# A slot-ordered selective scan on one core: the gate put behind a scan, the D skip and one sum put a slot later

## The chip, the cores and the metric

The kernel runs on one core of a Trainium2 chip. The metric is device time in microseconds (us) of one execution. Before the change the median of three runs is 5206.82 us (5206.63 to 5207.61). One further execution was profiled; every duration below that is not a run time comes from its trace.

## The reference, cut to what matters

Two images of 256 channels by 4096 positions go through two layers. Layer 0 holds one Mamba block (256 inner channels); layer 1 holds two, one forward and one over the reversed positions (512 inner channels each), and then a mixture of 8 expert networks. The heart of every Mamba block is a recurrence with 16 states for each channel, a sum over the states, a skip by `D`, and a gate by `silu(z)`:

```
def step(h, inp):
    dt_t, B_t, C_t, x_t = inp
    h = h * jnp.exp(dt_t[..., None] * A) + (dt_t * x_t)[..., None] * B_t[:, None, :]
    y = jnp.einsum('bds,bs->bd', h, C_t)
    return (h, y)
...
y = sw(ys) + xc * D
out = y * _silu(z) @ W_out
```

All arithmetic is float32.

## The kernel before, in words

**Tiling.** Positions are cut into 8 chunks of 512 (`T`). A channel tile is 128 channels, so a chunk of layer 0 has `nj` = 2 tiles and one of layer 1 has `nj` = 4. The 16 states of a tile are handled in four groups of four. One such group is a *quad*: a buffer `bq` of 128 partitions (32 channels times 4 states) by four channel sets by 512 positions. Six `bq` buffers exist (`bqp`), so quad m takes the buffer of quad m - 6. A quad is worked in two halves `h` of 128x1024; each half is a *slot*. Eight quads, that is 16 slots and two channel tiles, make a *block*. The whole loop (L1011 and below) has 640 quads, 1280 slots, 80 blocks: 8 blocks for layer 0 of image 0, 16 for the forward and 16 for the backward block of layer 1, and the same again for image 1. Slots are counted 0 to 15 inside a block here; slot 2n + h is the pair (n, h) of the code.

**What one quad needs.** GpSimd (POOL) multiplies the replicated `dt*x` by `B` into `bq` (`emit_b`, L654). ScalarE (ACT) puts `exp(dt*A)` of each half into a PSUM tile `da` (`emit_decay`, L664, two instructions of 128x512; there are two `da` tiles, so the one of slot s takes the place of slot s - 2). VectorE (DVE) scans the half (`emit_scan`, L690). The product with `C` is made by DVE right behind the scan (`emit_times_c`, L699) or, for quads n = 0, 2, 5 and in every second block half of n = 4, by POOL (`emit_times_c_quad`, L714 and L715; the two are called c0, c2, c5 and h4 here). TensorE (PE) sums the four states with the constant `stack` (`emit_sum`, L723) into the one PSUM bank `y` of the tile. Before the first sum of a tile the bank is opened with `D` times `xc` (`emit_skip`, L730); after its last sum DVE multiplies it into `sz`, the gate (`emit_gate`, L742). As `ps_y` has one buffer, a tile's skip must wait for the gate of the tile before it. `emit_diagonal` (L735) makes the skip's weights on ACT in slots 0 and 8.

**What sets the order.** Each engine works in the order in which the loop emits, which is kept by hand (`in_order`). In each slot the loop emits: the DMA list `sp`; the gate, when the slot is (1, 0) or (5, 0); the skip, when it is (1, 1) or (5, 1); the PE list `pe`; the sums that the table `SUMS` gives this slot; the PE list `pe2` (the experts); ACT's carry of the slot before (L709), the decay of the *next* slot (with its one-column join L675), and the list `act`; the list `dve0`; the scan; the list `dve`; the product with `C`; POOL's entries from `POOL_AT`. The lists hold the next chunk's preparation: input projections (`xs`, `z`, L414), convolution (L452) whose result goes through ACT's tanh (L461) and DVE's product (`xc`, L466), `dbc` (L481), `dt` (L501 to L523), and the finish of the chunk before, the output projection (`o`, L759 and L761). They share three PSUM banks (`psp`). In layer 0 the convolution stands in slot 12, the output projections in slots 7 and 8, and `xs` in slots 9 and 10.

**A planner** (`experts`, L847 and below) puts matmuls of the experts into slots where it reckons PE and ACT to have room; the cost that it takes for sums and skip of a slot is `sums_in`. What does not fit is done after the loop, in the last 680 us.

Of the kernel before, what the change touches and what calls it, by code (L numbers as in the profile page):

```python
# [61 lines left out]

POOL_HALF = (4, 0)

SUMS = {(0, 0): (-1,), (2, 0): (0, 1), (4, 0): (2, 3), (5, 1): (4,), (7, 0): (5, 6)}
POOL_AT = {0: "b3", 1: "c0 b4", 2: "b5", 3: "c2 b6", 4: "b7", 5: "h4 b8", 6: "c5 b9", 7: "b10"}
HUGE = 1e37

# [63 lines left out]
def hybrid_kernel(ctx: ExitStack, tc: tile.TileContext, a: dict, out: bass.AP):  # L132
# [53 lines left out]
    with ExitStack() as st:  # L186
# [394 lines left out]
        def at(g):  # L581

            i, jp, n = quads[g]
            return i, 2 * jp + n // SG, n % SG
# [48 lines left out]
        def flush(slot):  # L633
            for p in list(pending):
                if p[0] <= slot and (p[1] if len(p[1]) > 1 else p[1][0]) in cks[p[3]]:
                    pending.remove(p)
                    p[2]()
# [18 lines left out]
        def emit_decay(g, h):  # L656
            if g >= nq or ("rdt", at(g)[1]) not in cks[at(g)[0]]:
                return
            emit_join(g, h)
            i, j, sg = at(g)  # L660
            da[g, h] = ps_d.tile([P, 2, T], F32, tag="da", name=f"da_{g}_{h}")
            for k in range(2):
                q = 2 * h + k
                nc.scalar.activation(  # L664
                    da[g, h][:, k, :], cks[i]["rdt", j][:, q, :], AF.Exp,
                    scale=steps[i][0].w["a"][:, j, q * SG + sg : q * SG + sg + 1],
                )
# [12 lines left out]
        def on_pool(g, h):  # L680

            n = quads[g][2]
            return n in POOL_C or (n, h) == POOL_HALF and g // QN % 2

        def emit_scan(g, h):
            i, j, sg = at(g)
            job, c = steps[i]
            d = da[g, h].rearrange("p q t -> p (q t)")
            b = bq[g][:, 2 * h : 2 * h + 2, :].rearrange("p q t -> p (q t)")
            nc.vector.tensor_tensor_scan(  # L690
                b if on_pool(g, h) else d, d, b,
                job.h[:, j, sg, 2 * h : 2 * h + 1] if c else 0.0, ALU.mult, ALU.add,
            )
# [10 lines left out]
        def emit_carry(g, h):  # L704

            i, j, sg = at(g)
            d, two = da.pop((g, h)), slice(2 * h, 2 * h + 2)
            if not on_pool(g, h):
                nc.scalar.copy(steps[i][0].h[:, j, sg, two], d[:, :, T - 1])  # L709
# [10 lines left out]
        def emit_sum(g):  # L720
            i, j, sg = at(g)
            for q in range(SG):
                nc.tensor.matmul(  # L723
                    y[i, j][q * CG : (q + 1) * CG, :], stack, bq[g][:, q, :],
                    start=False, stop=(sg == SG - 1),
                )

        def emit_skip(i, j):
            y[i, j] = ps_y.tile([P, T], F32, tag="y", name=f"y_{i}_{j}")
            nc.tensor.matmul(y[i, j], diag.pop((i, j)), cks[i]["xc", j], start=True, stop=False)  # L730
# [9 lines left out]
        def emit_gate(i, j):  # L740
            sz = cks[i]["sz", j]
            nc.vector.scalar_tensor_tensor(sz, y.pop((i, j)), 0.5, sz, ALU.mult, ALU.mult)  # L742
# [104 lines left out]
        def experts():  # L847

            last = 2 * nq - 6
            banks = sorted(sl.banks, key=lambda r: r[0])  # L850

            def fits(slot):

                at = sum(b[0] <= slot for b in banks)
                both = banks[:at] + [(slot, slot + 1, 0)] + banks[at:]
                return all(
                    both[k - 3][1] + both[k][2] <= both[k][0] for k in range(max(3, at - 2), min(len(both), at + 4))
                    if at in range(k - 3, k + 1)
                )

            def sums_in(slot):
                n, h = divmod(slot % 16, 2)
                return 1.25 * len(SUMS.get((n, h), ())) + (1 if (n, h) in ((1, 1), (5, 1)) else 0)

            todo = [(at, b, c, e) for at, b, c in sorted(ready) for e in range(E)]
            behind = act_behind = 0.0
            times = [[], [], []]

            def follows(l):

                k, m = divmod(len(times[l]), KC)
                if k == len(todo):
                    return None
                waits = [(l - 1, k * KC + 1, 2)] if l else []
                if m:
                    waits.append((l, k * KC, 0))
                elif k:

                    waits.append((l, k * KC - 1, 6 if l == 0 and todo[k][-1] == 0 else 5))
                    if l < 2:  # L880
                        waits.append((l + 1, k * KC - 1, 0))
                if any(n >= len(times[w]) for w, n, _ in waits):
                    return None
                return max([todo[k][0] + 3] + [times[w][n] + d for w, n, d in waits])

            for slot in range(last):
                behind = max(0.0, behind) + sl.products.get(slot, 0) + sums_in(slot) - PE_ROOM
                act_behind = max(0.0, act_behind) + sl.acts.get(slot + 1, 0) - ACT_ROOM
                for l in (2, 1, 1, 0, 0):
                    at = follows(l)  # L890
                    if at is None or slot < at:
                        continue
                    if behind + 2 > PE_BEHIND or act_behind + 1.3 > ACT_BEHIND or not fits(slot):
                        break
                    banks.insert(sum(b[0] <= slot for b in banks), (slot, slot + 1, 0))
                    times[l].append(slot)
                    behind += 2
                    act_behind += 1 if l == 2 else 1.3
            put = [
                (*item[1:], [times[l][k * KC + m] for l in range(3) for m in range(KC)])  # L900
                for k, item in enumerate(todo) if (k + 1) * KC <= len(times[2])
            ]
            emit_experts(put)
# [106 lines left out]
        done = []  # L1010
        for g in range(nq):  # L1011
            i, jp, n = quads[g]
            for h in range(2):
                slot = 2 * g + h
                sl.run(slot, "sp")
                flush(slot)

                if (n, h) in ((1, 0), (5, 0)) and done:
                    emit_gate(*done.pop(0))

                if (n, h) in ((1, 1), (5, 1)):
                    emit_skip(i, 2 * jp + n // SG)
                sl.run(slot, "pe")
                for m in SUMS.get((n, h), ()):
                    if g - n + m >= 0:
                        emit_sum(g - n + m)
                sl.run(slot, "pe2")
                if (n, h) in ((0, 0), (4, 0)) and g:
                    done.append(at(g - 1)[:2])

                if slot:
                    emit_carry(*divmod(slot - 1, 2))
                emit_decay(*divmod(slot + 1, 2))
                if (n, h) in ((0, 0), (4, 0)):
                    emit_diagonal(i, 2 * jp + n // SG)
                sl.run(slot, "act")

                sl.run(slot, "dve0")
                emit_scan(g, h)
                sl.run(slot, "dve")  # L1040
                if not on_pool(g, h):
                    emit_times_c(g, h)

                if h == 0:
                    for what in POOL_AT.get(n, "").split():
                        m = g - n + int(what[1:])
                        if what[0] == "c":
                            emit_times_c_quad(m)
                        elif what[0] == "h":
                            if on_pool(m, 0):  # L1050
                                emit_times_c_quad(m, SG // 2)
                        else:
                            want_b(m)
                sl.run(slot, "pool")
            in_order()
# [6 lines left out]
    with ExitStack() as st:  # L1062
# [5 lines left out]
        n, x, y, acc, wts, wb, lt, w_dram = {}, {}, {}, {}, {}, {}, {}, {}  # L1068
# [192 lines left out]
        done = {i: 0 for i in rest}  # L1261
        count = {i: sum(p[1] == i for p in pairs) for i in rest}
        for at, (b, i, e) in enumerate(pairs):
# [3 lines left out]
            h = layer(n[b, i], 0, e, f"{i}_{e}_{b}")  # L1267
            h = layer(h, 1, e, f"{i}_{e}_{b}")
# [122 lines left out]
```

## Time and profile before

| what | value |
|---|---|
| median of three runs | 5206.82 us |
| the profiled execution's own time | 5213.06 us |
| its span, first to last instruction | 5211.3 us |
| busy in the span: DVE, POOL, PE, ACT | 4584.8, 4410.2, 4298.0, 3681.8 us |
| last gate of the loop | 4531.6 us after the start |
| gates (L742): number, median duration, DVE idle before them | 160, 0.682 us, 45.6 us |
| scans (L690) with a carried state: mean duration | 2.35 us |
| product by `B` on POOL (L654): number, mean | 640, 4.542 us |
| mean granted clock of TensorE | 0.918 |

In what follows, a line of a timeline gives the start in us from the first instruction, the duration in us, the engine, the line of the kernel, the operation, what it writes and reads, the shapes, how many instructions were merged (x), and in brackets how long the engine stood idle before it and what ended that. A line of waits gives who waited for whom, the sum in us, how many times, and the longest. A line by stretches gives from:to, its length, the busy us of PE, PE's weight loads, DVE, ACT and POOL with their numbers of instructions, then PE's granted clock, the DMA share and GB/s.

### The profile page before, as it was taken

The page shows a single profiled execution, that of the slowest core. Times are in us where ns is not written, and L with a number is a line of the kernel's source. Part 1 is how long each engine was busy: PE and PEld are TensorE (multiplying, and loading weights), DVE is VectorE, ACT ScalarE, POOL GpSimd, SP SyncE. Part 2 cuts the span into 40 slices and gives each one's busy share as a digit, 9 for nine tenths or more (in the row PEclk, how much of TensorE's full clock was granted, in tenths as well). Part 3 has the DMA queues.
Part 4 walks back from the last instruction along what each step waited for, and adds up shares of the span by engine and source line. Part 5 has one row for each costly group of instructions (what it writes and reads, how often), then busy time and mean ns, then how long its engine had stood idle before and what let it go on. Part 6 is the DMA issues. An engine that isn't in the chain of part 4 may idle for free. (4 is left out here: it accounts for less than half of the span.)

```text
span 5211.3 us, 47295 instructions
## 1 busy us (share of the span) xinstructions
PE 4298.0 (82%) x14920; PEld 1488.2 (29%) x14920; DVE 4584.8 (88%) x3083; ACT 3681.8 (71%) x7462; POOL 4410.2 (85%) x1438
## 2 busy tenths in 40 slices
PE   5777666766668888888888888888999989689999
PEld 1222212222222333332222332322333333234444
DVE  6998999999999999998989999999999999746333
ACT  5777777777767888887887888788788888522332
POOL 5998999999999999998989999999999999611010
PEclk8778888888889999999999999999999999899999
DMA  4444433344434554555555544445544455354322
GB/s 175 146 165 164 162 134 126 130 156 148 140 135 159 187 186 166 181 174 185 197 177 182 178 169 169 164 159 194 184 171 163 163 184 178 115 194 154 111 103 77
DMA packets 314731, 834.47 MB, mean 160 GB/s; under 512 B 35240, under 2 KB 102064, under 8 KB 272496
## 3 DMA queue, kind: packets, MB, share of 16 engines
q1 hardware_dynamic: 310768, 806.15, 44.5%
q0 software_dynamic: 3712, 25.30, 1.2%
q8 instruction: 118, 1.93, 0.1%
q14 instruction: 133, 1.09, 0.1%
HBM read 647.18 MB, written 184.16 MB: 160 GB/s over the span
## 5 line engine op out<-in xcount | busy, mean ns | idle before, releaser
L654 POOL TENSOR_TENSOR bq<-rxdt,bc 128x2048 f32<-128x2048 f32 x640 | 2892.9, 4542 | 34.8 <-issue 17.4
L664 ACT ACTIVATE da<-rdt,w_a 128x512 f32<-128x512 f32 x2560 | 1756.8, 686 | 113.6 <-DVE bq L690 67.8
L690 DVE TENSOR_TENSOR_SCAN da<-da,h_state,bq 128x1024 f32<-128x1024 f32 x664 | 1559.5, 2349 | 38.7 <-ACT da L664 27.3
L715 POOL TENSOR_TENSOR bq<-bq,bc 128x2048 f32<-128x2048 f32 (+1 forms) x280 | 1179.6, 4213 | 22.5
L723 PE MATMUL y<-bq,stack 128*32 128x512 f32 x5120 | 779.4, 687 | 362.1 <-POOL bq L715 337.2
L690 DVE TENSOR_TENSOR_SCAN bq<-da,h_state,bq 128x1024 f32<-128x1024 f32 x456 | 1052.3, 2337 | 27.9 <-ACT da L664 27.8
L699 DVE TENSOR_TENSOR bq<-da,bc 128x1024 f32<-128x1024 f32 x760 | 928.2, 1221 | 18.7
L912 PE MATMUL e<-eh,ew 128*128 128x512 f32 x1184 | 582.4, 621 | 60.5 <-DVE sp L513 20.5
L709 ACT COPY h_state<-da 128x2 f32<-128x2 f32 x759 | 119.3, 157 | 687.5 <-DVE bq L699 685.4
L675 ACT ACTIVATE bq<-h_state,bq,a 128x1 f32<-128x1 f32 x1120 | 429.9, 384 | 0.5
L723 PEld LDWEIGHTS y<-bq,stack 128*32 128x32 f32 x5120 | 144.9, 118 | 935.1 <-POOL bq L715 458.6
L1205 ACT ACTIVATE h<-hp,of,sc 128x512 f32<-128x512 f32 x216 | 167.7, 777 | 345.0 <-PE hp L1201 328.5
L414 PE MATMUL xs<-nx,w_in 128*128 128x512 f32 x640 | 320.1, 630 | 36.8 <-DVE xc L466 20.7
L414 PE MATMUL z<-nx,w_in 128*128 128x512 f32 x640 | 326.2, 638 | 23.7 <-DVE sp L513 16.9
L912 PEld LDWEIGHTS e<-eh,ew 128*128 128x128 f32 x1184 | 212.4, 193 | 422.3 <-issue 194.5
L912 PE MATMUL e<-en,ew 128*128 128x512 f32 x592 | 290.5, 622 | 47.3 <-DVE fcen L809 21.5
L452 PE MATMUL conv<-xs,w_conv 64*64 64x512 f32 x2560 | 320.5, 608 | 4.6 <-DVE sp L513 3.7
L761 PE MATMUL o<-sz,w_out 128*128 128x512 f32 x640 | 306.7, 620 | 0.0
L923 ACT ACTIVATE eh<-e,of,sc 128x512 f32<-128x512 f32 x296 | 223.7, 769 | 37.9 <-PE e L912 36.7
L517 POOL TENSOR_TENSOR xdt<-sp,xc 128x512 f32<-128x512 f32 x160 | 203.4, 1275 | 53.3 <-DVE sp L513 53.3
L501 PE MATMUL dt<-dbc,w_dt 64*128 64x512 f32 x320 | 197.2, 701 | 44.5 <-ACT dbc L488 27.7
L730 PE MATMUL y<-xc,w_d 128*128 128x512 f32 x320 | 181.0, 649 | 60.8 <-DVE sz L742 51.3
(138 smaller groups left out, 5043.0 us busy)
## 6 DMA issues: line engine op xcount, KB each, us to landing
rxdt<-xdtd SPq DMA_DIRECT2D x160, 1024.0 KB, 6.4
rdt<-dtd SPq DMA_DIRECT2D x160, 1024.0 KB, 6.3
bc<-bcd SPq DMA_DIRECT2D x384, 256.0 KB, 3.2
dtd<-sp SPq DMA_DIRECT2D x160, 256.0 KB, 3.5
xdtd<-xdt SPq DMA_DIRECT2D x160, 256.0 KB, 3.4
ew<-in_W SPq DMA_DIRECT2D x148, 256.0 KB, 4.8
u<-eu SPq DMA_DIRECT2D x74, 512.0 KB, 3.5
u<-u SPq DMA_DIRECT2D x74, 512.0 KB, 4.0
```

Source lines behind the costliest of these rows:

```text
L414: nc.tensor.matmul(ps, job.w["in", half][:, k, j * P : (j + 1) * P], rhs, start=(k == 0), stop=(k == KC - 1),)
L452: nc.tensor.matmul(v[r][64 * col : 64 * col + 64, :], job.w["conv"][rows, 2 * jp + j, k, :], ck["xs", jp][rows, j, k : k + T] if k < 4 els ...
L654: nc.gpsimd.tensor_tensor(bq[g], ck["rxdt", j], over_groups(ck["bc", 0, sg]), ALU.mult)
L664: nc.scalar.activation(da[g, h][:, k, :], cks[i]["rdt", j][:, q, :], AF.Exp, scale=steps[i][0].w["a"][:, j, q * SG + sg : q * SG + sg + 1],)
L675: nc.scalar.activation(bq[g][:, q, 0:1], job.h[:, j, sg, q : q + 1], AF.Identity, scale=cks[i]["a0", j][:, h, sg : sg + 1], bias=bq[g][:, ...
L690: nc.vector.tensor_tensor_scan(b if on_pool(g, h) else d, d, b, job.h[:, j, sg, 2 * h : 2 * h + 1] if c else 0.0, ALU.mult, ALU.add,)
L699: nc.vector.tensor_tensor(bq[g][:, two, :], d, cks[i]["bc", 1, sg].rearrange("p (o t) -> p o t", o=1).to_broadcast([P, 2, T]), ALU.mult,)
L715: nc.gpsimd.tensor_tensor(b, b, cks[i]["bc", 1, sg].rearrange("p (o t) -> p o t", o=1).to_broadcast([P, groups, T]), ALU.mult,)
L723: nc.tensor.matmul(y[i, j][q * CG : (q + 1) * CG, :], stack, bq[g][:, q, :], start=False, stop=(sg == SG - 1),)
L761: nc.tensor.matmul(v[m], job.w["out"][:, j, m * P : (m + 1) * P], ck["sz", j], start=False, stop=(j == job.nj - 1),)
L912: nc.tensor.matmul(ps, ew[l][:, k, m * P : (m + 1) * P], key[x][:, k, :], start=(k == 0), stop=(k == KC - 1),)
L923: nc.scalar.activation(key[dst][:, m, :], key["ps", l, m], AF.Relu, bias=of[:, l, e, m : m + 1], scale=sc[:, l, e, m : m + 1],)
```

## The change

Three edits. The gate is emitted behind the scan of its slot instead of ahead of it. The skip is emitted in slots 4 and 12 instead of 3 and 11; the sums 0 and 1 of a tile, which stood in slot 4 before, now follow it in the same slot. The sum of quad 4 goes from slot 11 to slot 12, where it follows the list `pe`. The planner's `sums_in` is told of it. Nothing is computed differently, and no instruction is added or taken away.

```
-SUMS = {(0, 0): (-1,), (2, 0): (0, 1), (4, 0): (2, 3), (5, 1): (4,), (7, 0): (5, 6)}
+SUMS = {(0, 0): (-1,), (2, 0): (0, 1), (4, 0): (2, 3), (6, 0): (4,), (7, 0): (5, 6)}
...
-                return 1.25 * len(SUMS.get((n, h), ())) + (1 if (n, h) in ((1, 1), (5, 1)) else 0)
+                return 1.25 * len(SUMS.get((n, h), ())) + (1 if (n, h) in ((2, 0), (6, 0)) else 0)
...
-                if (n, h) in ((1, 0), (5, 0)) and done:
-                    emit_gate(*done.pop(0))
-
-                if (n, h) in ((1, 1), (5, 1)):
+                if (n, h) in ((2, 0), (6, 0)):
                     emit_skip(i, 2 * jp + n // SG)
                 sl.run(slot, "pe")
...
                 sl.run(slot, "dve0")
                 emit_scan(g, h)
+
+                if (n, h) in ((1, 0), (5, 0)) and done:
+                    emit_gate(*done.pop(0))
                 sl.run(slot, "dve")
                 if not on_pool(g, h):
                     emit_times_c(g, h)
```

## Prediction

> **What bounds the kernel now.** I read the profile by stretches first, cut where the layers change: 60 to 538 us is layer 0 of image 0, 538 to 1411 the forward block of layer 1, 2302 to 2780 layer 0 of image 1, 3659 to 4530 the last backward block.
>
> ```profile
> 60.00:538.00 478.00, 334.89 (x1166) 96.93 (x1168) 433.91 (x283) 349.64 (x719) 443.55 (x143) 0.79 0.47 164
> 538.00:1411.00 873.00, 602.19 (x2312) 184.63 (x2308) 855.23 (x556) 635.90 (x1340) 868.30 (x278) 0.85 0.39 140
> ...
> 2302.00:2780.00 478.00, 414.13 (x1447) 136.70 (x1447) 431.69 (x281) 392.44 (x786) 430.41 (x140) 0.95 0.55 191
> ...
> 3659.00:4530.00 871.00, 771.42 (x2784) 267.35 (x2784) 846.46 (x540) 689.63 (x1419) 846.09 (x267) 0.95 0.48 165
> ```
>
> The third and fifth busy figures (DVE, POOL) are the ones to read. In the second line POOL is busy 868.3 of 873 us: it sets the pace, and DVE time saved there is worth nothing. In both layer 0 stretches DVE and POOL are each idle for 34 to 48 us of 478, so they wait for each other. Then the waits of the whole span:
>
> ```profile
> POOL h_state L714 <- DVE bq L690: 73.0, 43, 5.0
> ...
> PE y L730 <- DVE sz L742: 51.3, 30, 7.2
> ...
> DVE sz L742 <- PE y L723: 45.4, 37, 4.7
> ```
>
> The last line is what the change is about: DVE stands 45.4 us ahead of the gate, for the sums. The first is what it could pay: POOL stands 73 us for a scan of DVE. By stretch, the gate's wait is 16.5 and 8.1 us in the two layer 0 stretches (always or mostly the gate of slot 10), 9.6 us where POOL is full, and 9.0 us in the other three, mostly 0.2 us at a time. POOL's wait in layer 0 is 15.8 and 24.5 us. So the case lies in layer 0. One such gate on DVE, ACT and PE:
>
> ```profile
> 214.31 1.21 DVE L699 TENSOR_TENSOR bq<-da,bc 128x1024 f32<-128x1024 f32 x1
> 218.25 0.69 DVE L742 SCALAR_TENSOR_TENSOR sz<-y,sz 128x512 f32<-128x512 f32 x1 [2.73 <-PE y L723]
> 218.86 4.58 DVE L690 TENSOR_TENSOR_SCAN bq<-da,h_state,bq 128x1024 f32<-128x1024 f32 x2
> 223.36 2.33 DVE L690 TENSOR_TENSOR_SCAN da<-da,h_state,bq 128x1024 f32<-128x1024 f32 x1
> ```
> ```profile
> 216.82 1.41 ACT L664 ACTIVATE da<-rdt,w_a 128x512 f32<-128x512 f32 x2
> 218.17 0.18 ACT L435 COPY xs<-kept 128x6 f32<-128x6 f32 x1
> 220.10 0.59 ACT L436 COPY xs<-xs 128x512 f32<-128x512 f32 x1 [1.75 <-PE xs L414]
> 220.58 0.39 ACT L675 ACTIVATE bq<-h_state,bq,a 128x1 f32<-128x1 f32 x1
> 221.23 1.42 ACT L664 ACTIVATE da<-rdt,w_a 128x512 f32<-128x512 f32 x2 [0.27 <-DVE bq L690]
> ```
> ```profile
> 210.47 2.07 PE L759 MATMUL o<-xr,ident 128*128 128x512 f32 x2 [8.63 <-DVE sz L543]
> ...
> 215.89 2.26 PE L723 MATMUL y<-bq,stack 128*32 128x512 f32 x16
> 218.08 3.70 PE L414 MATMUL xs<-nx,w_in 128*128 128x512 f32 x8
> ```
>
> PE was held 8.63 us at the output projection until DVE freed a bank, so its sums 2 and 3 end at 218.15, and the gate, scans 10, 11 and 12 follow one another from there.
>
> **What the Trainium skill says.** "TensorE: Matmul & The Clock Gate", section on the array (engine queue depths): ScalarE and VectorE take their queues strictly in order. The trace agrees: for 2.73 us scan 10 stands behind the gate although its `da` was there. "SBUF — State Buffer", section on the two separate sides: DVE and GpSimd share a port pair, which a DVE operation with two SBUF inputs locks against GpSimd. The gate has one input in PSUM and one in SBUF, so its new place should not slow POOL; the product by `B` takes 4.489 to 4.586 us in all 640 cases, which shows no such collisions now. "VectorE: DVE Perf Modes", section on the DRAIN: the next operation does not start until the pipe is empty. The trace differs: an independent operation starts 0.08 us before the reported end of the one ahead, one that reads its result 0.03 us after it.
>
> **The change part by part.**
>
> *Gate behind the scan, slot 10.* In the example the product of slot 9 ends at 215.52. Scan 10 (`da` ready at about 213.3) would run from 215.45 to 217.8; the gate, still held by the sums, from 218.25 to 218.93; scan 11 (`da` ready at 218.23) from 218.85, against 221.1 now: 2.25 us earlier. So min(wait, 2.35) or so returns at scan 11. What is late next is scan 12. Its `da` needs the buffer of scan 10, now early, but on ACT it stands behind the copy of `xs` at 220.10, which waits for PE, and PE has not moved: copy to 220.69, join to 220.97, decay to 222.4. Scan 12 starts at about 222.4 against 223.36, so 0.96 us of the 2.73 stays. The gates with 2.13 to 2.73 us of wait have the same neighbours, so I take 1.0 us for each (four in layer 0 of image 0, less one where a layer-norm subtraction waits for PE at the same place: 3 times 1.0), 1.4 less 0.3 for the one with 1.37, and the two waits of 0.34 whole. The first block's 4.73 us counts as nothing: POOL does not wait for a scan in it. Layer 0 of image 0: 3.0 + 1.1 + 0.3 = 4.4.
>
> *Gate behind the scan, slot 2.* Without a wait the gate now fills the pause between a scan and its own product: 0.03 + 0.08 = 0.11 us less each time. Against that, scan 2 wants its `da` 0.6 us sooner. Where ACT is late it cannot have it: in image 1's layer 0 the scan ahead of the gate at 2428.5 ends at 2428.57 and ACT's decay at 2429.20, which the gate covers now; uncovered, the product of the slot starts 0.41 us later. I went through all 79 such gates with the starts and ends of the trace: in 33 `da` comes after DVE is free, which would cost 4.0 us in sum. The sum outside the POOL-bound stretch, waits of the gate included, is -0.6 + 0.4 in layer 0 of image 0, -1.5 + 2.0 in that of image 1, and -7 in layer 1, of which over half lies where POOL waits for no scan; I keep 3.
>
> *Skip and sum 4, slot 12.* In layer 0 the convolution of slot 12 stood behind skip and sum 4 of slot 11; now only behind the skip, so it ends one sum (1.06 us) earlier. That matters where `xc` waits for it:
>
> ```profile
> 2584.53 1.23 DVE L699 TENSOR_TENSOR bq<-da,bc 128x1024 f32<-128x1024 f32 x1
> 2587.70 0.69 DVE L466 SCALAR_TENSOR_TENSOR xc<-thx,conv 128x512 f32<-128x512 f32 x1 [1.95 <-ACT thx L461]
> ```
>
> In image 1's layer 0 this wait occurs 7 times, 8.3 us; with at most 1.0 each I count 6. It stands behind the gates of the same blocks and takes their gain and most of the 2.0 us loss in, so the gates there add only 0.5. In image 0 there is one (4.7 us): 1.0.
>
> *Nothing.* The skip's own wait for the gate: in slot 4 sum 0 waits for c0, which starts only after scan 1 and takes 4.5 us, while the gate is done 3.0 us after scan 1; in slot 12 it is hidden by the lists of slot 11, or by the wait for c5. If that cover is gone, PE loses at most one scan, 2.35 us, at such a gate. Sum 4 frees the buffer that POOL's product for quad 10 takes; in the tightest block I found (2571 us) sum 4 would end near 2587.0 and that product starts at 2588.0. No DMA is issued by what is moved. SP's and POOL's orders of work are otherwise those of before, except that the planner moves 178 of 444 expert steps, most by 1 to 6 slots, with the same number of experts. I can't price that from the trace: between -5 and +5 us, taken as 0.
>
> *Sum.* 4.4 + 0.2 + 1.0 (layer 0, image 0), 6 + 0.5 (image 1), 3 (layer 1): 15 us. The profiled execution took 5213.06 us, span 5211.3 and 1.8 around it; it would take 5198. It lay 6.2 us above the median, so on the median's footing 5206.8 - 15 = 5191 to 5192; I say 5191.
>
> **The rivals.** A measurement of this kernel can tell about 0.2% (10.4 us) from no change; the bounds are 5196.4 and 5217.2.
>
> A, the forecast, its own range 5184 to 5199.
>
> B, the waits return whole: ACT's `xs` copy is not what comes next. Then min(wait, 2.35) over the layer 0 gates of slot 10 is 13 + 5 us, and with 6 to 7 from the convolution and 3 from layer 1, 27: 5180, or 5174 with a lucky planner. For it: POOL's waits there, 40 us, have room. Against: the ACT lines above.
>
> C, nothing to measure: POOL sets the pace in layer 0 too, or the 0.4 us losses eat the gains; 3 to 8 us: about 5202. For it: gates, convolution and c0 waits are links of one loop that gains only what its slowest path gains.
>
> D, slower: the gate was the cover of ACT's late decay in slot 2. Some 60 of the 80 such gates lie where POOL is not full; if each costs the 0.41 us seen, that is +25, less 9 from slot 10: about 5223. It decides from the point where `da` comes more than 0.11 us after DVE is free; now that is so in 30 of the 79, mostly by little, and an expert step moved onto ACT's slot 1 would make it more.
>
> That the change doesn't do what it says can't be: the order of the built kernel has every gate behind its scan and every skip and sum moved.
>
> **How the numbers follow.** A 0.45, B 0.15, C 0.25, D 0.15. Faster by over 0.2%: most of A and all of B, 0.55. Within: the rest of A and C, 0.30. Slower: 0.15. The range takes in A, B and C with the planner's bounds and ends at the foot of D: 5174 to 5217.
>
> **What would show it.** Right: the gate's wait falls from 45 us to under 12; c5's wait for scan 11 in layer 0 goes; scan 12 waits for ACT there about 1 us a time (B: it doesn't); the convolution's tanh waits less. Wrong: new DVE waits for `da` at scan 2 summing over 20 us (D), a POOL wait for the sums at quad 10's product, or layer 0 stretches that keep 478 us (C).

## The result and the profile after

The changed kernel takes 5183.82 us (median of five runs, 5182.55 to 5186.02), the kernel before in the same comparison 5206.82 us. The ratio is 0.9953, with a 95% interval from 0.994 to 0.9965: 23 us faster, where 15 had been forecast. The profiled execution spans 5181.8 us.

The same four stretches as before the change, by time from the start (length, then the busy us of PE, weight loads, DVE, ACT and POOL):

```profile
61.00:525.00 464.00, 324.34 (x1164) 102.96 (x1164) 433.46 (x282) 347.61 (x717) 440.68 (x142) 0.81 0.50 168
525.00:1398.00 873.00, 608.21 (x2310) 182.38 (x2312) 855.79 (x556) 635.88 (x1341) 868.50 (x278) 0.82 0.40 140
2287.00:2755.00 468.00, 403.31 (x1438) 134.05 (x1437) 430.67 (x282) 390.86 (x784) 430.92 (x140) 0.96 0.57 194
3633.00:4500.00 867.00, 770.45 (x2780) 263.02 (x2778) 842.70 (x539) 689.92 (x1419) 845.36 (x267) 0.95 0.48 165
```

DVE and POOL are busy about as long as before (433.5 and 440.7 us in the first stretch, 433.9 and 443.6 then). What shrinks is the time in which they are kept waiting, in the two layer 0 stretches: 477.0 to 464.4 and 478.3 to 468.0 us, cut at the first scans. The second line, where POOL is busy 868.5 of 873 us, stays. The waits of the whole span that answer to the three shown before, and ACT's for a scan, the latter once more as it was before:

```profile
POOL h_state L714 <- DVE bq L690: 54.9, 38, 5.4
PE y L730 <- DVE sz L742: 55.4, 23, 3.3
ACT da L664 <- DVE bq L690: 53.0, 64, 2.0
DVE sz L742 <- PE y L723: 7.2, 8, 2.0
```
```profile
ACT da L664 <- DVE bq L690: 67.8, 83, 2.0
```

The gate's wait fell from 45.4 to 7.2 us, POOL's for scans from 73.0 to 54.9. The skip's wait for the gate did not fall (51.3 before). The third line of the four is one that the prediction never looked at: ACT's decay waiting for a scan, 67.8 us before, 53.0 now. The same gate of slot 10, in the third block, on DVE and ACT:

```profile
210.49 1.21 DVE L699 TENSOR_TENSOR bq<-da,bc 128x1024 f32<-128x1024 f32 x1
211.62 2.34 DVE L690 TENSOR_TENSOR_SCAN bq<-da,h_state,bq 128x1024 f32<-128x1024 f32 x1
213.96 0.69 DVE L742 SCALAR_TENSOR_TENSOR sz<-y,sz 128x512 f32<-128x512 f32 x1
214.56 2.34 DVE L690 TENSOR_TENSOR_SCAN bq<-da,h_state,bq 128x1024 f32<-128x1024 f32 x1
218.08 2.36 DVE L690 TENSOR_TENSOR_SCAN da<-da,h_state,bq 128x1024 f32<-128x1024 f32 x1 [1.18 <-POOL bq L654]
```
```profile
215.81 0.59 ACT L436 COPY xs<-xs 128x512 f32<-128x512 f32 x1 [1.41 <-PE xs L414]
216.30 0.39 ACT L675 ACTIVATE bq<-h_state,bq,a 128x1 f32<-128x1 f32 x1
216.59 1.41 ACT L664 ACTIVATE da<-rdt,w_a 128x512 f32<-128x512 f32 x2
```

Scan 10 no longer stands behind the gate, and the gate no longer waits. Scan 12 now waits 1.18 us. The bracket names POOL, but ACT's decay ends at 218.00, 0.08 before the scan; the decay is late because the copy of `xs` ahead of it waited for PE. That is the step that the prediction worked out.

### A cause outside the diff

In layer 0 of image 0 the gain (12.6 us) is twice what the order was priced at (5.6), and part of it lies at scans 5 and 6, which the diff doesn't touch. The fifth block on ACT, before and then after (the decay of slot 5 is the second of each):

```profile
307.17 0.14 ACT L709 COPY h_state<-da 128x2 f32<-128x2 f32 x1
307.21 0.39 ACT L675 ACTIVATE bq<-h_state,bq,a 128x1 f32<-128x1 f32 x1
309.36 1.42 ACT L664 ACTIVATE da<-rdt,w_a 128x512 f32<-128x512 f32 x2 [1.76 <-DVE bq L690]
```
```profile
300.05 0.14 ACT L709 COPY h_state<-da 128x2 f32<-128x2 f32 x1
300.09 0.39 ACT L675 ACTIVATE bq<-h_state,bq,a 128x1 f32<-128x1 f32 x1
300.38 1.40 ACT L664 ACTIVATE da<-rdt,w_a 128x512 f32<-128x512 f32 x2
```

and scans 4, 5 and 6 on DVE before, then scans 5 and 6 after:

```profile
306.99 2.34 DVE L690 TENSOR_TENSOR_SCAN bq<-da,h_state,bq 128x1024 f32<-128x1024 f32 x1
309.24 0.67 DVE L513 SCALAR_TENSOR_TENSOR sp<-dt,sp 128x512 f32<-128x512 f32 x1
310.81 2.35 DVE L690 TENSOR_TENSOR_SCAN bq<-da,h_state,bq 128x1024 f32<-128x1024 f32 x1 [0.90 <-ACT da L664]
313.08 0.67 DVE L513 SCALAR_TENSOR_TENSOR sp<-dt,sp 128x512 f32<-128x512 f32 x1
314.38 2.36 DVE L690 TENSOR_TENSOR_SCAN da<-da,h_state,bq 128x1024 f32<-128x1024 f32 x1 [0.64 <-issue]
```
```profile
302.71 2.34 DVE L690 TENSOR_TENSOR_SCAN bq<-da,h_state,bq 128x1024 f32<-128x1024 f32 x1
305.55 2.35 DVE L690 TENSOR_TENSOR_SCAN da<-da,h_state,bq 128x1024 f32<-128x1024 f32 x1
```

The decay of slot 5 waits until 309.36, the end of scan 4 (306.99 + 2.34 = 309.33). With two `da` tiles in turn it would wait for scan 3. So here the tile of slot 5 lies where that of slot 4 lay, and the sentence in the description of the kernel (the tile of slot s takes the place of slot s - 2) is not always true. The addresses in the built programs say the same: of 1280 `da` tiles, 30 take the buffer of the slot just before in the kernel before, 23 in the changed one. Such a tile is called a *repeat* below. Both kernels ask for two buffers under one name (L661); which tile gets which is settled when the program is built, and moving other instructions changed it. Eight repeats went (slots 21, 37, 53, 69 and 85, all in layer 0 of image 0, and 625, 869 and 933), one came (1269). Each of the five cost DVE about 0.90 us at scan 5, and four of them (all but slot 21) about 0.64 more at scan 6: 7.0 us that no step of the prediction holds.

Theory 1: the order gave about 15 us as predicted, the five buffers about 8. Theory 2: all 23 come from the order, the gate's wait being returned nearly whole. The first four runs fix the buffers by hand.

### The profile page after: what moved, and what is told of

It is laid out like the page before. It is cut to its first block, busy times and chain, and to the rows that moved or that the text cites. A ratio compares the mean times of both kernels' runs of the same rounds, so it can differ in the third digit from the quotient of the medians.

```text
span 5181.8 us, 47299 instructions
## 1 busy us (share of the span) xinstructions
PE 4292.9 (83%) x14920; PEld 1483.9 (29%) x14920; DVE 4577.8 (88%) x3083; ACT 3681.3 (71%) x7462; POOL 4410.4 (85%) x1438
## 5 line engine op out<-in xcount | busy, mean ns | idle before, releaser
L723 PE MATMUL y<-bq,stack 128*32 128x512 f32 x5120 | 765.4, 691 | 347.4 <-POOL bq L715 324.1
L730 PE MATMUL y<-xc,w_d 128*128 128x512 f32 x320 | 193.6, 689 | 66.0 <-DVE sz L742 55.4
```

What stands on the lines that cost most here:

```text
L723: nc.tensor.matmul(y[i, j][q * CG : (q + 1) * CG, :], stack, bq[g][:, q, :], start=False, stop=(sg == SG - 1),)
```

## The experiments

Times of e1 to e11 are compared with runs of the kernel before on the same chip (medians 5210.1 to 5210.83 us); the changed kernel's -23.0 is from the first comparison, against 5206.82. The stretches are those of each kernel's profiled execution, cut at the first scans of the layers; "layer 1" is the sum of its four stretches. They come from single executions, so their sum can lie some us off the median's difference (the profiled execution of before was itself 6.2 us above its median, that of e1 6.8 us).

| kernel | median less before's, us | layer 0, image 0 | layer 0, image 1 | layer 1 |
|---|---|---|---|---|
| before | 0 | 477.0 | 478.3 | 3512.3 |
| changed | -23.0 | 464.4 | 468.0 | 3507.0 |
| e1 order of before, buffers of after | -12.0 | 465.8 | 478.8 | 3515.4 |
| e2 order of after, buffers of before | -17.9 | 470.5 | 471.3 | 3509.2 |
| e3 order of before, buffers in turn | -21.9 | 464.4 | 467.4 | 3509.5 |
| e4 order of after, buffers in turn | -35.7 | 464.0 | 464.6 | 3502.1 |
| e5 gate only | +9.2 | 471.7 | 478.5 | 3526.6 |
| e6 skip and sum only | +9.3 | 471.6 | 472.6 | 3527.7 |
| e7 order of after, old plan | -18.4 | 466.8 | 471.9 | 3506.3 |
| e8 order of after, `xs` copy later | -21.1 | 463.0 | 471.7 | 3511.9 |
| e9 second half of the block only | +3.3 | 468.9 | 471.7 | 3527.2 |
| e10 first half of the block only | -1.9 | 474.7 | 475.6 | 3511.5 |
| e11 order of after, in turn, copy later | -38.9 | 455.8 | 464.4 | 3502.5 |

e5 to e10 have the buffers of before, so they compare with e2. In e1, e2 and e5 to e10 a line of the helper shifts the numbers by one or two (scan L692, sum L725, skip L732, gate L744).

**e1 and e2: buffers and order apart.** e1 is the kernel before with the two tiles given by a list, here that of the slots that repeat in the changed kernel; e2 is the changed kernel with the list of before.

```
+REPEATS = (5, 25, 57, 89, 101, 357, 629, 633, ..., 1061, 1269)
...
-            da[g, h] = ps_d.tile([P, 2, T], F32, tag="da", name=f"da_{g}_{h}")
+            at_buf = (2 * g + h + sum(r <= 2 * g + h for r in REPEATS)) % 2
+            da[g, h] = ps_d.tile([P, 2, T], F32, tag=f"da{at_buf}", name=f"da_{g}_{h}", bufs=1)
```

> The order of before, but each da tile takes the PSUM buffer that it has in the changed kernel (23 tiles in place of 30 take the buffer of the slot just before them). Theory 1 (the 23 us are some 15 from the new order and some 8 from five da tiles of slot 5 in layer 0 of image 0 that no longer take the buffer of slot 4): 5199 us, and the layer 0 stretch of image 0 about 8 us shorter. Theory 2 (all of it is the order, the gate's wait comes back whole): 5207, no change.

> The order of the changed kernel with the da buffers of before. Theory 1: 5191 to 5192 us, with scan 5 waiting 0.9 us for its da again in five more blocks. Theory 2: 5184, as the changed kernel.

e1 took 5198.83 us against 5210.83, ratio 0.9978 (0.9972 to 0.9985): the buffers alone give 12.0 us; in the trace the stretch that shrinks is layer 0 of image 0, by 11.2. e2 took 5192.97, ratio 0.9962 (0.9948 to 0.9976): the order with the buffers of before gives 17.9. Theory 2 falls by e1, which it had at no change; e2 alone would not refute it, as its interval (12.5 to 27.1 us) takes in 23. In e2 the waits of scan 5 for its `da` in layer 0 of image 0 are back at 7.6 us, as before, against 3.1 in the changed kernel. Theory 1 stands with the buffers dearer than thought. In layer 0 of image 0 the two do not add: 11.2 and 6.5 apart, 12.6 together. A likely reason is that both shorten the same loop of DVE, ACT and PE.

The list itself is a change of form (two names with one buffer each in place of one name with two). The old order with the list of before was not run. In layer 0 of image 1, where both lists are the same, e1 takes 478.8 us against 478.3, so the form shows no effect there.

**e3 and e4: no repeats at all.** One name for each half, so the tiles take turns:

```
-            da[g, h] = ps_d.tile([P, 2, T], F32, tag="da", name=f"da_{g}_{h}")
+            da[g, h] = ps_d.tile([P, 2, T], F32, tag=f"da{h}", name=f"da_{g}_{h}", bufs=1)
```

> The order of before, the two da buffers taken strictly in turn, so that no da waits for the scan just before it. Theory 1: DVE's waits at scans 5, 6 and 9 of some 30 blocks (about 25 us in layer 0, 10 in layer 1) go, and over half of that is time: 5186 to 5195 us. Theory 2: POOL or the gate takes that time up, 5203 to 5207.

> The changed kernel with the two da buffers strictly in turn. Theory 1: the order is worth about 15 us whatever the buffers, so about 15 below the kernel of before with buffers in turn, 5170 to 5178 us. Theory 2: 23 below it, and within 5 of the changed kernel, 5179 to 5184.

e3 took 5188.93, ratio 0.9956 (0.9944 to 0.9969), e4 5175.1, ratio 0.9933 (0.992 to 0.9945). One line, in the old order, is worth about as much as the whole change. The order on top of it (e3 to e4) is worth 13.8 us. ACT's wait for a scan in e3:

```profile
ACT da L664 <- DVE bq L690: 30.7, 59, 1.4
```

67.8 us of it had stood on the page of the kernel before, with a longest of 2.0 us. The Trainium skill, "Perfetto Trace Analysis", section "Optimization Strategy", says that the same gap repeating on the engine that should be saturated can mean a lack of SBUF or PSUM for the next tile, naming the buffer count. The trace agrees in the symptom (0.90 us at scan 5 in six of the eight blocks of layer 0, image 0, before, and in none of them in e3), but not in the cause: the count was enough, the turn was wrong.

**e5 and e6: one edit alone.** e5 moves only the gate; e6 moves only the skip and sum 4, and tells the planner.

```
-                if (n, h) in ((1, 0), (5, 0)) and done:
-                    emit_gate(*done.pop(0))
...
                 emit_scan(g, h)
+
+                if (n, h) in ((1, 0), (5, 0)) and done:
+                    emit_gate(*done.pop(0))
```
```
-SUMS = {(0, 0): (-1,), (2, 0): (0, 1), (4, 0): (2, 3), (5, 1): (4,), (7, 0): (5, 6)}
+SUMS = {(0, 0): (-1,), (2, 0): (0, 1), (4, 0): (2, 3), (6, 0): (4,), (7, 0): (5, 6)}
...
-                if (n, h) in ((1, 1), (5, 1)):
+                if (n, h) in ((2, 0), (6, 0)):
```

> The gate behind the scan alone; skip, sums and planner are those of the kernel before, and so are the buffers of every da tile. Theory 1 (the parts as the prediction priced them): the stretch of layer 0, image 0 falls by 4 to 5 us, that of image 1 by 1 to 2, layer 1 by 3 in sum: 7 to 9 us less than before, half of what the whole order gave (17.9). Theory 2 (the gate is the whole change, the skip and sum 4 only make room for it): 15 to 18 us less. Theory 3 (without the skip moved, the skip of slot 3 waits for a gate that now comes a scan later, and the sums with it): 0 to 4 us less, and PE's waits for the gate grow.

> The skip in slots 4 and 12, sum 4 in slot 12 and the planner's costs of the changed kernel; the gate stays ahead of the scan, and every da tile has the buffer that it has in the kernel before. Theory 1: 6 to 9 us less than before, nearly all in layer 0 of image 1, where the waits of xc for ACT's tanh fall from 8.3 to about 4 us; layer 0 of image 0 about 1 us less. Theory 2: within 3 us of before.

Every theory missed. e5 took 5219.29, ratio 1.0015 (1.0007 to 1.0023); e6 5219.38, ratio 1.0017 (1.0009 to 1.0025). Each edit alone makes the kernel slower by 9 us; together they make it 18 faster. In layer 0 they help (5.1 us for e5, all in image 0, and 11.1 for e6 over both images), in layer 1 each costs 14 to 15 us. The waits of e5 over the whole span:

```profile
PE y L732 <- DVE sz L744: 162.9, 73, 7.3
...
DVE xc L467 <- ACT thx L462: 70.3, 46, 14.1
```

and one case on PE in its layer 1:

```profile
4024.38 3.60 PE L914 MATMUL e<-en,ew 128*128 128x512 f32 x8
4029.27 1.12 PE L732 MATMUL y<-xc,w_d 128*128 128x512 f32 x2 [1.30 <-DVE sz L744]
4030.33 3.66 PE L453 MATMUL conv<-xs,w_conv 64*64 64x512 f32 x32
```

The gate came a scan later, but the skip stayed in slot 11, ahead of the convolution. PE waits 1.30 us for the gate, the convolution is late, and `xc` waits for its tanh (0.55 us in this case; 70.3 us in all, 37.7 before). By stretch, in the three of layer 1 where POOL is not full, `xc` waits 22.6 us for its tanh against 2.1 before, and the gates 2.0 against 11.1: 11.4 us more, of the 14.3 that layer 1 lost; the stretch where POOL is full lost nothing (873.2 us, 873.3 before). So Theory 3 of e5 had the mechanism, but not its size.

e6 loses in another place. Its gates, still ahead of the scan, wait longer:

```profile
DVE sz L744 <- PE y L725: 56.9, 38, 4.0
```

45.4 us of it had stood on the page of the kernel before. In the same three stretches the gates wait 27.1 us against 11.1, nearly all of it in slot 2. That is 16.0 more, about what layer 1 lost (15.4); e9 below shows why.

**e7: the planner.** The order of after, but the planner is told where before had the sums.

```
-                return 1.25 * len(SUMS.get((n, h), ())) + (1 if (n, h) in ((2, 0), (6, 0)) else 0)
+                sums = {(0, 0): 1, (2, 0): 2, (4, 0): 2, (5, 1): 1, (7, 0): 2}
+                return 1.25 * sums.get((n, h), 0) + (1 if (n, h) in ((1, 1), (5, 1)) else 0)
```

> The whole order of the changed kernel with the buffers of before, but the planner reckons the sums where the kernel before had them, so that only 20 of 444 expert steps differ from the kernel before (178 did). If the moved expert steps are worth nothing, it takes the time of the changed order with before's buffers (17.9 us less than before) within 4 us. If they gave part of the gain, it lies 5 us or more above that; if they cost, 5 us or more below.

5191.74 us, ratio 0.9963 (0.9951 to 0.9976), against 0.9962 for e2: the moved expert steps are worth nothing that these runs can tell, with intervals some 13 us wide.

**e8: the copy that keeps 1 us.**

```
-                return (0, "pe", pe), (1, "act", act)
+                return (0, "pe", pe), (2 if nj == 2 and j == 0 else 1, "act", act)
```

> The changed order with the buffers of before, and in layer 0 the first of ACT's two copies of xs emitted one slot later, so that it stands behind the decay of slot 12 and not ahead of it. If that copy is what keeps the 1 us of each gate's wait, as the prediction has it, the waits ahead of scan 12 (6.3 us in layer 0 of image 0, 1.2 in that of image 1) go, and the time falls by 3 to 6 us below the changed order alone, that is 21 to 24 us less than before. If scan 12 waits for something else (the product by B, the carry), the wait stays and the time is that of the changed order, 17.9 less. If the copy then holds something later in ACT's list, the time rises above that.

5189.0 us, ratio 0.9959 (0.9947 to 0.9972). The decay of slot 12 now goes ahead of the copy, and scan 12 has no wait:

```profile
214.78 1.42 ACT L666 ACTIVATE da<-rdt,w_a 128x512 f32<-128x512 f32 x2
216.13 0.18 ACT L436 COPY xs<-kept 128x6 f32<-128x6 f32 x1
216.21 0.58 ACT L437 COPY xs<-xs 128x512 f32<-128x512 f32 x1
```
```profile
215.24 2.34 DVE L692 TENSOR_TENSOR_SCAN bq<-da,h_state,bq 128x1024 f32<-128x1024 f32 x1
217.50 2.33 DVE L692 TENSOR_TENSOR_SCAN da<-da,h_state,bq 128x1024 f32<-128x1024 f32 x1
```

In e2 the waits of scan 12 sum to 4.0 us in layer 0 of image 0 and 1.5 in that of image 1; here they are gone in both. Layer 0 of image 0 falls by 7.5 us against e2. Of the whole, 3.2 us remain between the medians, within both intervals; the trace shows the mechanism, a gain in time clear of noise is not shown.

**e9 and e10: the halves of the block.** e9 moves the gate of slot 10, its skip and sum 4; e10 the gate of slot 2 and its skip. Both tell the planner. The edits of e9, with `SUMS` as in e6 (those of e10 mirror them, without the sum):

```
-                if (n, h) in ((1, 0), (5, 0)) and done:
+                if (n, h) == (1, 0) and done:
                     emit_gate(*done.pop(0))
-                if (n, h) in ((1, 1), (5, 1)):
+                if (n, h) in ((1, 1), (6, 0)):
...
                 emit_scan(g, h)
+                if (n, h) == (5, 0) and done:
+                    emit_gate(*done.pop(0))
```

> Only the block's second half is changed: the gate of slot 10 behind its scan, its skip from slot 11 to slot 12, sum 4 to slot 12; the first half (gate ahead of scan 2, skip in slot 3) is that of before, and so are the buffers of the da tiles. By the prediction's prices this half holds the slot-10 gates and the convolution: 4.4 + 1.0 in layer 0 of image 0, 6 in that of image 1, and some of the 3 in layer 1: 11 to 15 us less than before. Rival: what spoiled each edit alone (a gate and its skip that wait for each other through PE) sits in this half, and the first half brings the gain: 5 us less or nothing.

> Only the block's first half is changed: the gate of slot 2 behind its scan and its skip from slot 3 to slot 4; the second half is that of before, and so are the buffers of the da tiles. By the prediction's prices: 0.2 less in layer 0 of image 0, 1.5 less and 2.0 more in that of image 1, 3 less in layer 1: 2 to 5 us less than before. Rival (the prediction's case D): each gate of slot 2 covered a late da, 5 to 15 us more than before. If the halves add up, this one and the second half make 17.9.

e9: 5213.7 us, ratio 1.0007 (0.9999 to 1.0015). e10: 5208.44, ratio 0.9998 (0.999 to 1.0006). Neither differs from before by more than the noise, and the halves do not add up either: +1.4 against -17.9. By stretch the traces show where. The second half gains 14.7 us in layer 0 (11.4 were priced) and loses 14.9 in layer 1, where DVE waits at the gate of *slot 2*, in the last stretch 8.9 us against 2.9 before. One such gate, DVE before and then in e9:

```profile
4040.56 4.58 DVE L690 TENSOR_TENSOR_SCAN bq<-da,h_state,bq 128x1024 f32<-128x1024 f32 x2
4045.38 0.69 DVE L742 SCALAR_TENSOR_TENSOR sz<-y,sz 128x512 f32<-128x512 f32 x1 [0.24 <-PE y L723]
```
```profile
4036.52 4.58 DVE L692 TENSOR_TENSOR_SCAN bq<-da,h_state,bq 128x1024 f32<-128x1024 f32 x2
4042.40 0.69 DVE L744 SCALAR_TENSOR_TENSOR sz<-y,sz 128x512 f32<-128x512 f32 x1 [1.29 <-PE y L725]
```

and where PE loses that microsecond, in slots 10 to 12 of the block ahead, before and in e9:

```profile
4018.26 3.60 PE L912 MATMUL e<-en,ew 128*128 128x512 f32 x8
4021.70 1.02 PE L730 MATMUL y<-xc,w_d 128*128 128x512 f32 x2
4022.65 4.11 PE L452 MATMUL conv<-xs,w_conv 64*64 64x512 f32 x29
```
```profile
4014.23 3.60 PE L914 MATMUL e<-en,ew 128*128 128x512 f32 x8
4018.59 4.14 PE L453 MATMUL conv<-xs,w_conv 64*64 64x512 f32 x29 [0.76 <-ACT xs L437]
```

Before, the skip filled the time in which ACT copied `xs` for the convolution. With the skip behind it, PE stands 0.76 us and then works without a pause up to the tile's last sum in slot 0, which ends 3.55 us after the start of scan 1 instead of 2.49 (4042.33 less 4038.78; 4045.31 less 4042.82). The gate of slot 2, ahead of scan 2, waits for it. In the full change that gate stands behind scan 2, and 1 us of lateness is covered. The lines are one case; over the three stretches of layer 1 where POOL is not full, e9's gates wait 27.6 us against 11.1 before, as in e6. So the first half, which alone gives nothing clear of noise, is what makes the second half pay in layer 1.

**e11: all that gained.** e4 with the edit of e8.

> The changed order, the da tiles' two buffers strictly in turn, and the first xs copy of layer 0 behind the decay of slot 12: all three that gained. If the gains add up: 35.7 (order and buffers in turn) and 3 (copy) give 38 to 39 us less than before. If layer 0 of image 0 is at POOL's own time with the buffers in turn (464.0 us), the copy has nothing left to give there: 34 to 37 less.

5171.48 us, ratio 0.9925 (0.9913 to 0.9938): 38.9 us below before, the lowest median here. It lies 3.2 us below that of e4, as e8's copy had given over e2, and again within both intervals. In the trace layer 0 of image 0 goes from 464.0 to 455.8, so the thought that POOL itself held it at 464 falls. POOL is busy 440.78 us there now:

```profile
61.00:517.00 456.00, 321.47 (x1164) 97.69 (x1164) 434.32 (x282) 347.56 (x717) 440.78 (x142) 0.81 0.49 171
```

## Why the prediction was right, and where it failed

*The size, 15 us, was right for what it priced; its split over the stretches was right in part by luck.* With the buffers of before the order gives 17.9 us (interval 12.5 to 27.1, from the ratio), with buffers in turn 13.8 (e3 to e4), and with those of the changed kernel 11.0 (e1 to changed, over two comparisons). By stretch e2 shows 6.5 and 7.0 in the two layer 0 stretches where 5.6 and 6.5 were predicted, and 3.1 in layer 1 where 3 was. But in turn the same order gives 0.4, 2.8 and 7.4, from single traces: where it pays depends on the buffers, and no step of the prediction says so.

*Gate behind the scan, slot 10: right.* The gate's wait fell under the 12 us named. (Of the "two waits of 0.34" one lies in image 1; the sum rightly counts one.) Scan 12 is what came next, with 1.18 us in four of the blocks of image 0 and 1.55 in one, and e8 shows that the `xs` copy is its cause. Rival B (the waits return whole) is refuted for this order; its time, 5180, was nearly reached, but by the buffers.

*Slot 2: its loss was priced too low, and its part was not seen.* Scan 2 waits in 34 blocks, where 33 were counted, but the waits rose from 1.5 to 13.4 us over the kernel. Less the 1.5 of before and the 0.11 us a time that the prediction allows, that is about 8 us where 4.0 were priced. The waits stay under the 20 us that would have meant D. And that the moved gate covers a late last sum appears in no step.

*Skip and sum 4: right in image 1* (6 predicted, 5.7 in e6, tanh's wait in that layer 8.3 to 4.7 us in the changed kernel), too low in image 0 (1.0, and 5.4 in e6, where the gates wait 2.8 us less and `xc` 2.6).

*The part called "Nothing": the step that failed.* The skip's cover was examined from one side, its wait for the gate. "At most one scan, 2.35 us, at such a gate" holds in the case shown (1.30), but e5 pays such waits over and over (73 of PE, up to 7.3 us). What the skip itself covered on PE, ACT's copy ahead of the convolution, was not asked. Both were invisible in the sum because the full change hides each with the other. So the parts were priced as if they added up, and in layer 1 they don't: +14.3 (e5) and +15.4 (e6) give -3.1 together.

*Missing altogether: the buffers.* The order's share goes with c5's wait for scan 11 and the gate's; the 5 us and more beyond it come from `da` tiles, five of them in layer 0 of image 0, that stopped waiting for the scan just ahead. This term put the result at 5184 and not at 5189 to 5192. The planner at 0 fits e7. In layer 0 the c5 waits fell from 12.3 to 3.3 us and did not go to nothing.

What stays open: how the 12 us of e1 divide between the 7.0 us of idle removed and what the earlier scans let start earlier; and why, with the buffers in turn, the order gains 0.4 us in layer 0 of image 0 (e3 to e4) but 8.6 once the copy is moved as well. In those traces the gates' wait falls from 16.5 to 6.2 us and scan 12's rises from 0 to 6.3, which fits the copy as the common limit; no run without the new order has the copy moved.

## What to carry to other kernels

Where two buffers are meant to take turns, test it in the trace: a writer that waits for the reader of the tile just before, and not for the one before that, shows a repeat. Here a reordering that left the requests for these tiles as they were removed eight repeats and made one. Before a filler on one engine is moved, ask what it filled on both sides: what it waits for, and what the instruction behind it waits for. Price edits that shift the same chain together, since two that each cost 9 us alone saved 18 together here.

## What was not expected of the hardware and the program

A repeat of a PSUM tile costs DVE 0.90 us in each of the five blocks above, and 0.64 more in four of them, because a decay of 1.42 us can then not run beside the scan of 2.35 us ahead of it; 30 repeats in 1280 slots were worth 21.9 us (e3). The gate in its new place does not disturb POOL: the product by `B` has a mean of 4.543 us, 4.542 before.
